# Layer 3's two product groups moved next to each other, in the previous block's second half and behind the second block product of the next scores

## The chip, the cores and the metric

The kernel runs on one core of a Trainium2 chip. The core has TensorE for matmuls (PE; its weight loads are listed apart as PEld), VectorE (DVE), ScalarE (ACT), GpSimd (POOL) and SyncE (SP), which issues most DMA transfers. The engines run side by side, each through its own list of instructions in order, and wait for one another through semaphores. The metric is the device time of the whole kernel in microseconds (us), the median of some runs.

## What is computed

Eight images of 512 channels and 32x32 = 1024 positions go through four layers. In short (B = 8, C = 512, N = 1024):

```python
# layer 0: attention over channels reduced to 64, scaled by the largest singular value
x = Wv @ (h_x @ (f_x^T g_x / sigma)^T) + bv + x
# layer 1: group norm, then attention over 1024 positions with all 512 channels
h = group_norm(x, 32 groups)
q, k, v = wq @ h, wk @ h, wv @ h
x = x + wp @ (softmax(q^T k / sqrt(512)) applied to v)
# layer 2: attention over 1024 positions with 128 channels
t, p, g = split(W_w @ x)
x = batch_norm(Z_w @ (softmax(t^T p / sqrt(128)) applied to g)) + x
# layer 3: product of signs, then batch norm, residual, two slopes
a  = sign(x + rsign_bias)
Wb = sign(W) * mean(|W|, axis=1)
s  = batch_norm(Wb @ a) + x
t  = s - pr_shift
out = where(t > 0, t, pr_slope * t) + pr_bias
```

Layers 0 to 2 are computed in f32; the signs of layer 3 are f16.

## The kernel before

A first phase computes layer 0's small matrices for all images and folds weights together (`wu` from wq and wk, `wo` from wv and wp). Then the function `fast` is called once for each image, in the order 6, 7, 0 to 5 (`order`). One call does, on 128 partitions and in halves of 512 positions (`half(0)`, `half(1)`):

1. `scores1`: layer 1's scores and their exponentials, four rows of blocks
2. `make_v`, `values1`: layer 1's values and the attention's output
3. `project2`, `scores2`, `values2`, `close2`: layer 2. Next to it runs `make_u`, which already computes `ut`, a factor of the next image's scores
4. `leave`: layer 3 and the output, one half at a time

**Products of seven terms.** Large products are done with seven instead of eight block products (`seven`, lines 333 to 375). With the left factor's blocks A and the right factor's blocks B, the terms come in this order, one step of the generator each: A11·B11, S2·T2, S3·T3, S1·T1, A12·B21, S4·B22, A22·T4. The S and T are sums and differences of blocks, made on DVE beforehand (`sums_of`, `differences_of`). Each term is two f32 matmuls of 128x512 (four records in the trace) into a PSUM bank through line 388. A12·B21 adds to the bank of A11·B11, S4·B22 to that of S1·T1, A22·T4 to that of S3·T3, each once the first content has been taken out. The terms of one product make 7 steps. `scores1` has 4 such products, so the steps of its loop in `fast` count k from 0 to 27; `make_u` has 2.

In the trace these terms have the names of their factors. In `scores1`, the left factor `ut` gives `ut` for its own blocks (A11, A12, A22, and S3, which is written over A21) and `us` for S1, S2, S4; the right factor gives `h` for its own blocks and T3, and `hs` for T1, T2, T4. So the first steps of `scores1` read `ut,h` (A11·B11), `us,hs` (S2·T2), `ut,h` (S3·T3), `us,hs` (S1·T1), `ut,h` (A12·B21), then `us,h` (S4·B22) and `ut,hs` (A22·T4). Those of `make_u` read `wu`, `su` in place of `ut`, `us`.

**Where `us` comes from.** The last step of `make_u` calls `done`, which calls `sums_of` on `ut`: S1 (line 314), S2 (line 317), S3 (line 318) and S4 (line 319), four DVE instructions of 128x1024. Their inputs are evicted from PSUM by lines 341 (ACT), 345 and 347 (DVE), with an add on POOL (line 360).

**Layer 3.** `leave` (lines 679 to 752) makes for each half the signs `sg` (four ACT instructions, line 686) and then, for j = 0 and 1, one product group: four f16 matmuls of 128x512 into one bank (line 698). Two output channels are packed in each sum; ACT and DVE take them apart (line 709 on ACT, 710 and 711 on DVE), scale and add the residual (line 719, DVE), apply the two slopes (lines 741 and 742 on ACT, 749 on DVE), and two 256 KB transfers leave through SP. The generator yields once after each j; with `stop=True` it also yields after the signs.

**Where the groups stand.** In `fast`, half 0 goes through a loop with one step of `make_u` after each j (`fill()`), then `close2` of half 1 (line 675 on PE, line 677 on DVE), then half 1's signs:

```python
            for _ in leave(env, xt, dst, [0]):
                fill()
            close2(xt, att, 1)
            rest3.append(leave(env, xt, dst, [1], stop=True))
            next(rest3[0])
```

Half 1's two groups are left for the next image's scores. There, at k = 0, 2 and 4, one step of the waiting generator is taken; the third finds its end, and the next image's load is issued:

```python
            if rest3 and k % 2 == 0:
                if next(rest3[0], "end") == "end":
                    rest3.pop()
```

While `rest3` holds the generator, no step of the other background work (`chore`, layer 0's chains of small products, lines 1029, 1030 and 1061, in the first three images) is taken. The last image (`more` false) does its layer 3 in another way and isn't touched, nor is the first image's `scores1`, where `rest3` is empty. So there are seven changes from one image to the next with two groups of half 0 before them and two groups of half 1 after.

**The order on the engines.** PE's order is roughly the program's. A planner, which knows estimated durations, may move instructions between neighbours on each engine where no dependence forbids it. PSUM has 8 banks, which all these steps share (`bank`).

Of the kernel before, what the change touches and what calls it, by code (L numbers as in the profile page):

```python
# [85 lines left out]
def kernel(  # L86
# [36 lines left out]
    def bank():  # L123
        return psum["bank"].tile([P, HF], F32, tag="bank", name="bank")
# [9 lines left out]
    def load_x(b, split=False):  # L134
        t = xpool.tile([P, CC, N], F32, tag="x", name="xt")
        src = x[b].rearrange("(cc p) n -> p cc n", p=P)
        for cc in range(CC):
            for ns in [half(h) for h in range(NH)] if split and not cc else [slice(0, N)]:
                nc.sync.dma_start(out=t[:, cc, ns], in_=src[:, cc, ns])
        return t  # L140
# [164 lines left out]
    def quarters_of(t, rows, cols):  # L305

        return [t[:, rows[k], cols[m]] for m in range(2) for k in range(2)]

    def sums_of(a, more, queued=False):

        a11, a12, a21, a22 = a
        s1, s2, s4 = more
        tt = nc.vector.tensor_tensor
        first = tt(s1, a21, a22, ALU.add)
        if queued:
            tc.keep_in_program_order(first)
        tt(s2, s1, a11, ALU.subtract)  # L317
        tt(a21, a11, a21, ALU.subtract)
        tt(s4, a12, s2, ALU.subtract)
        return {"A11": a11, "A12": a12, "A22": a22, "S1": s1, "S2": s2, "S3": a21, "S4": s4}  # L320
# [147 lines left out]
    def split_h(env, ht):  # L468
        hs = env["big"].tile([P, 3, 2, HF], F32, tag="hs", name="hs")
        b = [ht[:, chunks[k], half(n)] for k in range(2) for n in range(2)]  # L470
        return differences_of(b, [hs[:, i] for i in range(3)])
# [44 lines left out]
    def scores1(env, hb, ua, es):  # L516

        scale = float(C) ** -0.5
        esum = env["small"].tile([P, N], F32, tag="esum", name="esum", bufs=1)
        for i in range(NTH):  # L520
            lo, hi = (env["e"].tile([P, N], F32, tag="e", name="e") for _ in range(2))
            es[i], es[NTH + i] = lo, hi
            term = product_of(
                lambda a, b, q, k: hb[b][:, k, bass.ts(i, P)],
                lambda a, b, q, k: ua[a][:, k, :],
            )

            yield from seven(
                term, lo[:, half(0)], hi[:, half(0)], lo[:, half(1)], hi[:, half(1)], exp=scale
            )  # L530
            nc.scalar.activation(lo[:, half(1)], lo[:, half(1)], AF.Exp, scale=scale)
            nc.scalar.activation(hi, hi, AF.Exp, scale=scale)
            if i == 0:
                nc.vector.tensor_tensor(esum, lo, hi, ALU.add)
            else:
                nc.vector.tensor_tensor(esum, esum, lo, ALU.add)
                nc.vector.tensor_tensor(esum, esum, hi, ALU.add)
        es.append(esum)
# [327 lines left out]
    def entering(n):  # L866

        b = order[n]
        f = load_f(b)

        def steps():
            while b // 2 not in ready:
                next(behind)
            if b % 2 == 0:
                for i in (b, b + 1):
                    pvs[i] = weights0(i)
            yield
            yield from enter(resident[b], f, pvs.pop(b), 2 if n else CC)

        return steps()  # L880

    rest3 = []
    verdict = []

    def fast(env, n, hb, ua):


        b = order[n]
        xt = resident.pop(b)
        more = n + 1 < B  # L890
        ahead = iter(())
        count = [0]

        def chore(every):
            count[0] += 1
            if count[0] % every == 0:
                next(behind, None)

        es = [None] * NT
        for k, _ in enumerate(scores1(env, hb, ua, es)):  # L900
            if rest3 and k % 2 == 0:
                if next(rest3[0], "end") == "end":
                    rest3.pop()
                    if more and order[n + 1] not in resident:
                        resident[order[n + 1]] = load_x(order[n + 1])
            if n == 0 and k == 2:
                weights["o"] = sums_of(quarters_of(wo, chunks, cols2), [so[:, i] for i in range(3)], True)
            if n == 0 and k == 6:
                tp = quarters_of(sbw["tpg"], chunks, [slice(0, P), slice(P, 2 * P)])
                weights["tp"] = sums_of(tp, [sp[:, i] for i in range(3)], True)  # L910
            if k == 8 and more:
                ahead = entering(n + 1)


            if k in (10, 13, 20, 27):
                next(ahead, None)
            if not rest3 and k not in (13, 14, 15, 20, 21, 22):
                chore(2)
        esum = es.pop()
        vt = env["big"].tile([P, NT, C], F32, tag="uv", name="vt")  # L920
        for k, _ in enumerate(make_v(hb, vt)):
            if k == 3:
                r = inverse_sums(env, esum, n)
            if k == 5:
                next(ahead, None)
            chore(2)
        for _ in ahead:
            pass
        scratch = env["big"].tile([P, 3, N], F32, tag="us", name="scratch")
        got = []  # L930
        steps = iter(())
        for k, _ in enumerate(values1(env, xt, vt, es, r, scratch)):
            chore(2)
            if k == 5 and more:
                nxt = resident[order[n + 1]]
                hb = split_h(env, normal(env, nxt))
        signs = None
        if more:
            steps = make_u(env, hb, got)
        else:  # L940
            signs = unpacked(env)

        def fill(k=1):
            for _ in range(k):
                next(steps, None)

        made = []
        for k, _ in enumerate(project2(env, xt, made)):
            fill(k > 5)
        tt, pt, gt = made  # L950
        es, esum = scores2(env, pt, tt, lambda t: fill(t % 2))
        banks, r = [None, None], None

        def values2(h, ts):
            if banks[h] is None:
                banks[h] = bank()
            for t in ts:
                mm(  # L958
                    out=banks[h],
                    lhsT=gt[:, t, :],  # L960
                    rhs=es[t][:, half(h)],
                    start=t == 0,
                    stop=t == NT - 1,
                )
            if t == NT - 1:
                att = env["small"].tile([P, HF], F32, tag="half_b", name="att")
                nc.vector.tensor_tensor(att, banks[h], r[:, h, :], ALU.mult)
                return att

        dst = channels(out[b])
        fill()
        values2(0, range(0, 2))
        if more:
            r = inverse_sums(env, esum, B + n)
            values2(0, range(2, NTH))
            att = values2(0, range(NTH, NT))
            values2(1, range(0, NTH))
            close2(xt, att, 0)  # L980
            att = values2(1, range(NTH, NT))
            fill()
            for _ in leave(env, xt, dst, [0]):
                fill()
            close2(xt, att, 1)
            rest3.append(leave(env, xt, dst, [1], stop=True))
            next(rest3[0])
            fill(2)
            for _ in steps:
                pass  # L990
        else:


            r = inverse_rows(env, esum, B + n)
            att = values2(0, range(2, NT))
            values2(1, range(0, 2))
            close2(xt, att, 0)
            values2(1, range(2, 6))
            before, after = leave(env, xt, dst, [0], signs), leave(env, xt, dst, [1], signs)
            count = count_bad(env)  # L1000
            next(count)
            next(before)
            next(before)
            att = values2(1, range(6, NT))
            next(before)
            close2(xt, att, 1)
            for _ in before:
                pass
            next(after)
            next(count)  # L1010
            for _ in after:
                pass

        return hb, got[0] if more else None
# [115 lines left out]
    env = {}  # L1130
# [105 lines left out]
    for b in range(B):  # L1236
        xt = load_x(b) if b else first
# [368 lines left out]
    with tc.If(verdict[0] > 0):  # L1606
        with (
# [5 lines left out]
            env = {"big": big, "e": epool, "small": small}  # L1613
# [4 lines left out]
            for b in range(B):  # L1618
                xt = load_x(b)
# [43 lines left out]
```

## Time and profile before

| | |
|---|---|
| time, median of 3 runs | 1902.76 us (1902.47 to 1903.66) |
| the profiled execution's own time | 1903.3 us |
| its span, first to last instruction | 1901.5 us |
| mean granted TensorE clock | 0.998 |
| f16 matmuls of line 698 on `sw` | 112, 28.7 us busy |
| 600.00 to 639.73 us | PE 39.73 busy, DVE 15.83, ACT 13.48 |
| 639.73 to 653.48 us (half 0's groups to the end of `make_u`) | PE 13.75 busy, DVE 12.52, ACT 10.46 |
| 653.48 to 672.00 us (start of the third image's scores) | PE 18.40 busy, DVE 17.68, ACT 10.63 |

All times inside a run are counted from the start of the span. A line of the timeline names start, length, engine, source line, operation, output and inputs, their shapes, how often it comes in a row, and in brackets how long the engine was idle before and for whom it waited. Matmuls overlap: in such a row the end of the last matmul lies behind the start of the next row, so that PE's time is read from start to start. A line of a group has the count, the busy time, the mean length of one in ns, and behind the second bar the idle time before it with what ended it. The chain of waits goes back from the last instruction to whatever released it each time.

### The profile page before, as it was taken

To read this page: it belongs to the slowest core of one execution; us is meant where nothing else is said; L and a number is where in the kernel's file an instruction comes from. 1 tells how busy PE (TensorE), PEld (TensorE's weight loads), DVE (VectorE), ACT (ScalarE), POOL (GpSimd) and SP (SyncE) were. 2 spreads that over 40 slices of the span, in tenths; PEclk is the share of its full clock that TensorE was granted. 3 is DMA by queue.
4 is the path that set the end of the run, shared out by engine and by line. 5 is a ranking of instruction groups with operands and counts; after the bars stand their busy time and mean duration, and the time that the engine had idled before them with its cause. 6 is when DMAs were issued, how large, how long until landed. Compare 5 with 4: busy or idle time off the path is not lost.

```text
span 1901.5 us, 16368 instructions
## 1 busy us (share of the span) xinstructions
PE 1879.4 (99%) x6178; PEld 976.9 (51%) x6178; DVE 1105.4 (58%) x1762; ACT 510.3 (27%) x811; POOL 224.3 (12%) x176
## 2 busy tenths in 40 slices
PE   9999999999999999999999999999999999999997
PEld 4366456544745447444645446544645455544653
DVE  3256576447664677437664675357753775466547
ACT  2142122134212432035202421134202521234013
POOL 0000101201121011200121001200130011101121
PEclk9999999999999999999999999999999999999999
DMA  8420000002000020002000110002000200000001
GB/s 321 159 78 6 0 7 12 1 16 84 17 1 1 34 72 12 1 12 89 17 1 0 45 61 12 1 22 78 12 0 12 89 12 0 1 33 22 12 0 47
DMA packets 25203, 66.52 MB, mean 35 GB/s; under 512 B 3552, under 2 KB 4764, under 8 KB 24476
## 3 DMA queue, kind: packets, MB, share of 16 engines
q1 hardware_dynamic: 24188, 64.96, 9.5%
q8 instruction: 51, 0.84, 0.2%
q10 hardware_dynamic: 864, 0.43, 0.1%
q14 instruction: 36, 0.29, 0.1%
q0 software_dynamic: 64, 0.00, 0.0%
HBM read 46.44 MB, written 18.94 MB: 34 GB/s over the span
## 4 chain that ended last, share of the span: by engine, by line
PE 92%; DVE 6%; issue 1%; ACT 1%; DMA 0%; POOL 0%; ACTq 0%; DVEq 0%
PE bank L388 42%; PE bank L557 20%; PE bank L958 6%; PE bank L806 6%; PE bank L1248 5%; PE bank L658 3%; PE bank L675 2%; PE bank L412 2%; PE wide L1288 1%; DVE both L749 1%; DVE both L719 1%; PE bank L1029 1%; PE wide L1342 1%; PE bank L1030 1%; PE bank L698 1%; DVE xt L677 1%
## 5 line engine op out<-in xcount | busy, mean ns | idle before, releaser
L557 PE MATMUL bank<-e,vt 128*128 128x512 f32 x768 | 334.2, 593 | 0.0
L557 PEld LDWEIGHTS bank<-e,vt 128*128 128x128 f32 x768 | 144.9, 190 | 174.8 <-issue 173.1
L388 PE MATMUL bank<-ut,h 128*128 128x512 f32 x384 | 182.3, 597 | 0.0
L345 DVE TENSOR_TENSOR e<-bank,e 128x512 f32<-128x512 f32 x128 | 87.7, 685 | 81.9 <-PE bank L388 81.7
L388 PE MATMUL bank<-us,hs 128*128 128x512 f32 x256 | 121.5, 597 | 1.3 <-DVE us L317 0.5
L388 PEld LDWEIGHTS bank<-ut,h 128*128 128x128 f32 x384 | 71.4, 190 | 95.6 <-issue 84.0
L958 PE MATMUL bank<-e,tpg 128*128 128x512 f32 x256 | 114.7, 595 | 0.0
L806 PE MATMUL bank<-tpg 128*128 128x512 f32 x256 | 114.6, 592 | 0.0
L813 ACT ACTIVATE e<-bank 128x512 f32<-128x512 f32 x128 | 76.4, 597 | 128.6 <-PE bank L806 128.6
L388 PE MATMUL bank<-wo,h 128*128 128x256 f32 x384 | 91.8, 382 | 0.0
L388 PE MATMUL bank<-h,wu 128*128 128x512 f32 x192 | 90.3, 593 | 0.7 <-ACT ut L350 0.7
L360 POOL TENSOR_TENSOR e<-e 128x512 f32<-128x512 f32 x32 | 43.3, 1354 | 403.9 <-ACT e L339 238.3
L818 DVE TENSOR_TENSOR esum<-esum,e 128x1024 f32<-128x1024 f32 x48 | 58.8, 1225 | 54.9 <-ACT e L813 54.9
L345 DVE TENSOR_TENSOR vt<-bank,vt 128x512 f32<-128x512 f32 x64 | 44.0, 688 | 68.9 <-PE bank L388 68.5
L806 PEld LDWEIGHTS bank<-tpg 128*128 128x128 f32 x256 | 48.6, 190 | 60.7 <-issue 60.5
L958 PEld LDWEIGHTS bank<-e,tpg 128*128 128x128 f32 x256 | 48.1, 190 | 60.4 <-issue 60.3
L360 POOL TENSOR_TENSOR ut<-ut 128x512 f32<-128x512 f32 x16 | 21.8, 1361 | 473.3 <-ACT ut L341 473.3
L388 PEld LDWEIGHTS bank<-wo,h 128*128 128x128 f32 x384 | 71.6, 190 | 11.5 <-issue 2.5
L388 PEld LDWEIGHTS bank<-us,hs 128*128 128x128 f32 x256 | 47.1, 190 | 54.9 <-issue 48.3
L686 ACT ACTIVATE sg<-xt,rb 128x512 f16<-128x512 f32 x64 | 45.0, 718 | 100.6 <-DVE xt L677 97.1
L1248 PE MATMUL bank<-xt,fg 128*64 128x512 f32 x256 | 59.1, 609 | 4.5 <-DMA fg<-in_w_fg 4.5
L658 PEld LDWEIGHTS bank<-tpg,xt 128*128 128x128 f32 x512 | 59.5, 192 | 7.2 <-issue 7.2
(330 smaller groups left out, 2974.0 us busy)
## 6 DMA issues: line engine op xcount, KB each, us to landing
xt<-in_x SPq DMA_DIRECT2D x55, 512.0 KB
out<-both SPq DMA_DIRECT2D x63, 256.0 KB
rfull<-r_dram SPq DMA_DIRECT2D x15, 512.0 KB
f_dram<-f SPq DMA_DIRECT2D x8, 256.0 KB
fb<-f_dram SPq DMA_DIRECT2D x8, 256.0 KB
w<-in_w SPq DMA_DIRECT2D x1, 1024.0 KB
q<-in_w_q SPq DMA_DIRECT2D x1, 1024.0 KB
k<-in_w_k SPq DMA_DIRECT2D x1, 1024.0 KB
```

The costliest lines, as they stand in the source:

```text
L345: nc.vector.tensor_tensor(dst, ps, u, ALU.add)
L360: nc.gpsimd.tensor_tensor(c22, c22, c12, ALU.add)
L388: mm(out=ps[:, q * w : (q + 1) * w], lhsT=lt(ka, kb, q, k), rhs=rhs(ka, kb, q, k), start=first and q == 0 and k == 0, stop=last and k == 1 ...
L412: mm(out=ps, lhsT=pv[side(h), bass.ts(oc, P)], rhs=f[side(h), :], start=True, stop=True,)
L557: mm(out=ps, lhsT=a[:, t, bass.ts(r_, P)], rhs=e[t], start=first and t == 0, stop=last and t == NTH - 1, skip_group_check=True,)
L658: mm(out=ps[:, i, :], lhsT=xt[:, cc, bass.ts(4 * h + i, P)], rhs=sbw["tpg"][:, cc, 2 * P : 3 * P], start=cc == 0, stop=cc == CC - 1,)
L686: nc.scalar.activation(sg[:, cc, :], xt[:, cc, half(h)], AF.Sign, bias=rb3[:, cc : cc + 1])
L806: mm(out=ps, lhsT=pt[:, 0, bass.ts(t, P)], rhs=tt[:, 0, half(h)], start=True, stop=True,)
L813: nc.scalar.activation(e[:, half(h)], ps, AF.Exp, scale=float(P) ** -0.5)
L818: nc.vector.tensor_tensor(esum, esum, e, ALU.add)
L958: mm(out=banks[h], lhsT=gt[:, t, :], rhs=es[t][:, half(h)], start=t == 0, stop=t == NT - 1,)
L1248: mm(out=banks[i][side(h), :], lhsT=w0[i][:, cc, :], rhs=xt[:, cc, half(h)], start=cc == 0, stop=cc == CC - 1,)
```

## The change

Two places in `fast` are changed. In the loop over `scores1`, the two groups of half 1 are both taken at k = 1, that is behind S2·T2 of the first row, instead of one at k = 0 (behind A11·B11) and one at k = 2 (behind S3·T3); at k = 4 the generator ends, as before. In the loop over `leave` of half 0, no step of `make_u` is taken after the first group and two after the second. No instruction is added or removed.

```diff
         for k, _ in enumerate(scores1(env, hb, ua, es)):
-            if rest3 and k % 2 == 0:
-                if next(rest3[0], "end") == "end":
+            if rest3 and k in (1, 4):
+                for _ in range(2):
+                    done = next(rest3[0], "end") == "end"
+                if done:
                     rest3.pop()
                     if more and order[n + 1] not in resident:
                         resident[order[n + 1]] = load_x(order[n + 1])
...
             fill()
-            for _ in leave(env, xt, dst, [0]):
-                fill()
+            for i, _ in enumerate(leave(env, xt, dst, [0])):
+                fill(2 * (i % 2))
             close2(xt, att, 1)
```

## The prediction

> **What bounds the kernel now.** I read the page first, then the chain of waits around one change of image, then the timelines of TensorE (PE) and VectorE (DVE) there, then the same place at the other six changes.
>
> From the page:
>
> ```profile
> PE 1879.4 (99%) x6178; PEld 976.9 (51%) x6178; DVE 1105.4 (58%) x1762; ACT 510.3 (27%) x811; POOL 224.3 (12%) x176
> PE 92%; DVE 6%; issue 1%; ACT 1%; DMA 0%; POOL 0%; ACTq 0%; DVEq 0%
> L388 PE MATMUL bank<-us,hs 128*128 128x512 f32 x256 | 121.5, 597 | 1.3 <-DVE us L317 0.5
> ```
>
> PE is busy for 99% of the span and carries 92% of the chain. There is next to nothing to win by shuffling PE work unless PE stands still somewhere, and the third line names such a place: products that read `us` and wait for the DVE sum of line 317. The chain of waits around the change from the second to the third image (start, length, what):
>
> ```profile
> 641.49 0.02 issue
> 641.52 0.44 DVE both L710
> ...
> 653.26 1.23 DVE us L314
> 654.49 0.06 DVE ut L347
> 654.55 0.52 issue
> 655.07 1.22 DVE us L317
> 656.29 0.04 issue
> 656.34 3.70 PE bank L388 x8
> ```
>
> Here the chain leaves PE for 15 us and runs through DVE without a break, from the first eviction of layer 3 (L710) to the sum S2 (L317); 0.05 us after S2 ends (656.28) PE starts S2·T2. The PE timeline at this place (start, length, then the group):
>
> ```profile
> 653.48 1.88 PE L388 MATMUL bank<-ut,h 128*128 128x512 f32 x4
> 655.19 1.03 PE L698 MATMUL bank<-sg,sw 128*128 128x512 f16 x4
> 656.34 1.98 PE L388 MATMUL bank<-us,hs 128*128 128x512 f32 x4
> 658.16 1.88 PE L388 MATMUL bank<-ut,h 128*128 128x512 f32 x4
> 659.88 1.03 PE L698 MATMUL bank<-sg,sw 128*128 128x512 f16 x4
> ```
>
> The ends in a row overlap the next start, so only starts count. A seven-product term takes 1.72 (653.48 to 655.19). A layer 3 group takes 0.86 undisturbed (a later query row: 659.88 to 660.74), and the terms and groups of the first half (639.73, 640.60, 642.31, 643.18) follow each other with no loss between f32 and f16. So 655.19 plus 0.86 is 656.06, and S2·T2 starts at 656.34: PE loses 0.28. The term itself then takes 1.82 instead of 1.72, another 0.10 for starting from rest. In other words, the layer 3 group covers 0.86 of a wait of 1.15 us for S2. The six other changes show the same: groups at 434.43, 872.24, 1081.37, 1289.25, 1498.39, 1706.27 and S2·T2 1.13 to 1.14 later each time.
>
> **What the Trainium skill says.** "TensorE: Matmul & The Clock Gate", Part 2, step 1, says that only weight loads may be pulled ahead and that matmuls stay in program order. The trace agrees: PE stands still before S2·T2 although S3·T3 and later groups follow it. So a group placed behind S2·T2 can't fill the wait. "SBUF — State Buffer", Who interferes with whom, says that a DVE instruction with two SBUF inputs and a GpSimd instruction that reads SBUF exclude each other, the later one blocking fully. The trace agrees: one L749 took 1.17 us at 648.94, beside the POOL add of 648.08, and its neighbour 0.74. "VectorE: DVE Perf Modes", The DRAIN you can't avoid, says that no instruction starts before the pipe is empty, but that one that isn't held starts earlier. The trace shows the second part, as follows.
>
> ```profile
> 643.18 1.41 DVE L719 SCALAR_TENSOR_TENSOR both<-both,sa,xt 128x512 f32<-128x512 f32 x2
> 644.51 0.42 DVE L710 TENSOR_SCALAR both<-both 128x512 f32<-128x512 f32 x1
> 644.96 0.69 DVE L711 SCALAR_TENSOR_TENSOR both<-both,bank 128x512 f32<-128x512 f32 x1
> 645.68 0.75 DVE L719 SCALAR_TENSOR_TENSOR both<-both,sa,xt 128x512 f32<-128x512 f32 x1
> ```
>
> An independent DVE instruction starts 0.08 before the end of the one ahead (643.18 + 1.41 = 644.59, the next at 644.51); one that reads its result starts 0.03 after (644.51 + 0.42 = 644.93, the next at 644.96). A dependence between neighbours costs 0.12.
>
> **Part 1, the first half (`leave` of half 0).** Before, PE runs group, S3·T3, group, S1·T1; after, group, group, S3·T3, S1·T1. The sum of PE's time is the same, the second group starts 1.72 earlier, S3·T3 0.86 later, and `close2` at 644.89 doesn't move. No instruction is added, the order of SP and POOL is the same, and no DMA changes place. Banks suffice: the eighth allocation back from each of these is evicted before. What changes is DVE's order (from the built program): L710, L711, then the second group's L710, L719 twice, L711, L345, L719, instead of L710, L711, L345, L719 twice, L710, L711, L719. The second L710's input is there in time: its ACT step can start 0.04 after the group's end (640.60 + 1.03 = 641.63), takes 0.69, so 642.36, and DVE comes to it at 642.58. Two of the three tight dependences (L710 to L711, L711 to L719) now have other work between them: 2 x 0.12 = 0.24 us less in a stretch in which DVE is full. The rest of the way to S2 keeps its order, and nothing else on it becomes late: L347 at 652.49 moves to 652.25 and needs a product ended at 651.92; the one at 654.41 needs 653.64. So S2 comes 0.24 earlier, S2·T2 at 656.10. Bounds: 0, if POOL holds L749 to the same time; 0.73, if everything but the products vanishes, since the second L347 can't start before 653.68 and it takes 0.66 + 1.22 + 0.05 to S2·T2 (655.61 at the earliest). I take 0.24, as the POOL add is itself behind an L719 that moves by 0.24.
>
> **Part 2, the scores (groups at steps 1 and 1 instead of 0 and 2).** A11·B11 ends its turn at 655.19 as before. Nothing now stands between it and S2·T2, so PE waits from 655.19 to 656.10, 0.91 instead of 0.28. That is 0.86 of cover gone and 0.24 regained, 0.62 lost. The two groups then run behind S2·T2 at full pace; their inputs `sg` are ready at 653.3. There are seven changes of image: 7 x 0.62 = 4.4 us. Nothing later gives this back, as PE has no wait of this size in the rest of an image. Step 4 ends the generator and starts the next load of x as before, so the added wait holds back only PE itself.
>
> **A second wait.** Late in the first row, S4·B22 accumulates into the bank of S1·T1, which ACT must first copy out (L339). In the images without a chain step in between, the order before is A12·B21, A22·T4, S4·B22:
>
> ```profile
> 1298.22 1.88 PE L388 MATMUL bank<-ut,hs 128*128 128x512 f32 x4
> 1299.94 1.88 PE L388 MATMUL bank<-us,h 128*128 128x512 f32 x4
> ...
> 1298.83 0.56 ACT L339 COPY e<-bank 128x512 f32<-128x512 f32 x1
> ```
>
> The copy ends at 1299.39, 0.55 before its user. After, the built order puts half of A22·T4 (0.86) behind S4·B22 in five of the seven images. Counted from S2·T2's start: two groups and four and a half terms (1.82 + 2 x 0.86 + 3 x 1.72 + 0.86) put S4·B22 at 9.56. L339 stands in ACT's queue behind two L709, L741, L741, two L742, L741; the first group ends at 2.85, L709 takes it to 3.57, DVE's L710, L711, L710, L719 to 5.75, and the first L741 to L339 takes 3.3 as now, so its end is 5.80 + 3.3 + 0.56 = 9.66, seen by PE at 9.72. That is 0.16 late, plus 0.10 for the start from rest: 0.26 x 5 = 1.3 us. Bounds: 0 (if I have a queue 0.2 too late) and 2.5 (0.5 each). In the other two images a chain step of 0.6 stands before and covers it.
>
> **Sum.** 4.4 + 1.3 = 5.7 us. The profiled execution took 1903.3 (its span is 1901.5), so 1909.0; against the median of 1902.76 that is 1908.4. What a measurement can tell from no change is about 0.2%, 3.8 us.
>
> **The rivals.**
> 1. Forecast, both waits: 1908.4. For it: S2 is ready 0.05 before its user at all seven places and PE can't pass it.
> 2. Only the first wait, the copy being in time: + 4.4, 1907.1. For it: 0.16 is a small margin over a dozen steps.
> 3. DVE saves nothing, POOL being what holds L749: 7 x 0.86 + 1.3 = + 7.3, 1910.1. Against: the POOL add starts after ACT's L341, which has the same L719s ahead of it.
> 4. DVE saves much more: the blocked L749 (0.43 long) escapes POOL. At its limit (0.73) the loss is 7 x 0.13 = + 0.9, 1903.7, no change that can be told.
> 5. Not slower, even faster: S2 is ready before A11·B11 ends. Then the present loss of 0.28 + 0.10 goes too: 7 x 0.38 = - 2.7, 1900.1. It decides from S2 ending at 655.14, 1.14 earlier than now; the second L347 forbids that by 0.42 (its end at 655.56 at the earliest) with the order built, so the dependence would have to be other than I read it. A gain over 0.2% would need still more.
>
> That the change doesn't do what it says is ruled out by the built order: eight f16 products in a row at all fourteen places.
>
> **How the numbers follow.** Chances: 0.58 for the first, 0.13 for the second, 0.10 for the third, 0.13 for the fourth (or anything else that ends within 3.8 of before), 0.06 for the fifth and what else could make it faster by over 0.2%. The first three are slower by over 0.2%, 0.81 together; the fourth is the same. The range goes from 1905.6 (a part of case 4, S2 0.45 earlier with no second wait: 7 x 0.41 = 2.9) to 1910.1, case 3.
>
> **What would show it.** Right: S2·T2 starts 0.8 to 1.0 after A11·B11's turn ends, at seven places, waiting for DVE L317, then groups in rows of eight; five waits for ACT L339 before `us,h`; L710 followed directly by another group's L710 on DVE. Wrong: S2 ending more than 0.5 earlier against the layer 3 groups of the first half, or PE losing time elsewhere.

## The result, and the profile after

The changed kernel takes 1908.64 us (median of 9 runs, 1908.23 to 1909.64); the kernel before, run beside it, 1903.54 us (9 runs, 1902.47 to 1904.22). The ratio is 1.0029 with a 95% interval of 1.0021 to 1.0037: slower by 5.1 us, with an interval that lies wholly above 0.2%. The profiled execution took 1908.4 us, its span is 1906.5.

The line of the page (section of the costliest groups) that named the wait, in the changed kernel: the idle time before the products that read `us` has grown from 1.3 to 5.8 us, all of it put down to the sum S2 of line 317.

```profile
L388 PE MATMUL bank<-us,hs 128*128 128x512 f32 x256 | 121.5, 597 | 5.8 <-DVE us L317 5.8
```

The PE timeline of the changed kernel at the change from the second to the third image (start, length, group):

```profile
639.68 1.89 PE L698 MATMUL bank<-sg,sw 128*128 128x512 f16 x8
...
653.42 1.88 PE L388 MATMUL bank<-ut,h 128*128 128x512 f32 x4
656.03 1.98 PE L388 MATMUL bank<-us,hs 128*128 128x512 f32 x4 [0.73 <-DVE us L317]
657.85 1.89 PE L698 MATMUL bank<-sg,sw 128*128 128x512 f16 x8
659.58 1.88 PE L388 MATMUL bank<-ut,h 128*128 128x512 f32 x4
```

The f16 groups now stand in rows of eight, at the same pace (657.85 to 659.58 is 1.73, two groups). A11·B11's turn ends 1.72 after 653.42, at 655.14; S2·T2 starts at 656.03. Read from start to start, PE stands for 0.89 us; the 0.73 in brackets is shorter, since the last matmul's drawn end runs 0.16 into the wait. Before it was 0.28. The VectorE side of the changed kernel, timeline of the first half's evictions and of the sum:

```profile
641.46 0.43 DVE L710 TENSOR_SCALAR both<-both 128x512 f32<-128x512 f32 x1 [0.82 <-ACT both L709]
641.92 0.69 DVE L711 SCALAR_TENSOR_TENSOR both<-both,bank 128x512 f32<-128x512 f32 x1
642.53 0.42 DVE L710 TENSOR_SCALAR both<-both 128x512 f32<-128x512 f32 x1
642.87 1.41 DVE L719 SCALAR_TENSOR_TENSOR both<-both,sa,xt 128x512 f32<-128x512 f32 x2
644.19 0.68 DVE L711 SCALAR_TENSOR_TENSOR both<-both,bank 128x512 f32<-128x512 f32 x1
644.79 0.68 DVE L345 TENSOR_TENSOR ut<-bank,ut 128x512 f32<-128x512 f32 x1
...
654.76 1.21 DVE L317 TENSOR_TENSOR us<-us,ut 128x1024 f32<-128x1024 f32 x1
```

From the first L710 to L317 it is 13.30 us, before 13.55 (641.52 to 655.07): 0.25 less. The whole of it is gained before the first L749 (4.58 us behind the first L710, before 4.83), the stretch in which the order is another one, and it is 0.25 there at all seven changes. Only the first L710 and L711 are still tight; behind the second L711, the next L719 now starts with L345 in between.

The second wait is there too. PE and then ACT in the changed kernel, at the change to the fifth image:

```profile
1090.83 1.88 PE L388 MATMUL bank<-ut,h 128*128 128x512 f32 x4
1092.55 1.02 PE L388 MATMUL bank<-ut,hs 128*128 128x512 f32 x2
1093.56 1.98 PE L388 MATMUL bank<-us,h 128*128 128x512 f32 x4
```

```profile
1092.34 0.70 ACT L741 ACTIVATE up<-both,cb 128x512 f32<-128x512 f32 x1
1092.95 0.56 ACT L339 COPY e<-bank 128x512 f32<-128x512 f32 x1
```

Half of A22·T4 (`ut,hs`) should take 0.86; S4·B22 (`us,h`) starts 1.01 after it, 0.05 after the copy of line 339 ends (1093.51). The trace puts 0.16 on this wait, at five changes, and the term it delays takes 1.98 instead of 1.88 in the drawing, another 0.10.

Where the 5 us went can be summed. From the first group of half 0 (418.97 before, 418.32 after) to the end of the span it is 1482.57 before and 1488.22 after: 5.66 us more. To the start of the last matmul alone it is 5.76; what follows that matmul (11.22 us before, 11.12 after) isn't touched by the change. The start of the program, which the change doesn't touch either, was 0.65 shorter in this execution, so the span shows only 5.0. Start to start, PE's stand before S2·T2 adds to 1.93 over the seven changes before and 6.38 after, 4.45 more; the wait for the copy adds 5 x (0.16 + 0.10) = 1.3. Together 5.75, against 5.76 up to the last matmul. No other wait between these points changed by more than 0.1.

### The profile page after: what moved, and what is told of

Same layout as the page of the kernel before. It is cut to its first block, busy times and chain, and to the rows that moved or that the text cites. A ratio compares the mean times of both kernels' runs of the same rounds, so it can differ in the third digit from the quotient of the medians.

```text
span 1906.5 us, 16382 instructions
## 1 busy us (share of the span) xinstructions
PE 1880.3 (99%) x6178; PEld 975.9 (51%) x6178; DVE 1104.6 (58%) x1762; ACT 513.3 (27%) x811; POOL 224.5 (12%) x176
## 4 chain that ended last, share of the span: by engine, by line
PE 92%; DVE 6%; ACT 1%; issue 1%; DMA 0%; POOL 0%; ACTq 0%; DVEq 0%
PE bank L388 42%; PE bank L557 20%; PE bank L960 6%; PE bank L806 6%; PE bank L1250 5%; PE bank L658 3%; PE bank L675 2%; PE bank L412 2%; PE wide L1290 1%; DVE both L749 1%; PE bank L698 1%; DVE both L719 1%; PE bank L1031 1%; PE wide L1344 1%; PE bank L1032 1%; DVE xt L677 1%
## 5 line engine op out<-in xcount | busy, mean ns | idle before, releaser
L345 DVE TENSOR_TENSOR e<-bank,e 128x512 f32<-128x512 f32 x128 | 87.8, 686 | 84.1 <-PE bank L388 84.0
L345 DVE TENSOR_TENSOR vt<-bank,vt 128x512 f32<-128x512 f32 x64 | 44.1, 689 | 68.8 <-PE bank L388 68.5
```

The costliest lines, as they stand in the source:

```text
L345: nc.vector.tensor_tensor(dst, ps, u, ALU.add)
```

## The experiments

All ratios are to the kernel before, run on the same chip beside them (1903.12 us for the first four runs, 1903.10 for the last two).

**Part 1 alone** (half 0's groups side by side, the scores as before):

```diff
-            if rest3 and k in (1, 4):
-                for _ in range(2):
-                    done = next(rest3[0], "end") == "end"
-                if done:
+            if rest3 and k % 2 == 0:
+                if next(rest3[0], "end") == "end":
```

Expected:

> Part 1 alone: the groups of half 0 back to back, those of half 1 at steps 0 and 2 of the scores as before. My account: S2 ends 0.24 us earlier at each of the seven changes (two tight dependences on VectorE gone), the group behind A11.B11 still covers 0.86, so the 0.28 of waiting before S2.T2 falls to about 0.04: 7 x 0.24 = 1.7 us faster than the kernel before (0.9991), ratio to it between 0.9985 and 0.9995; no wait of S4.B22 for the copy of line 339. Rival (part 1 itself costs, by a bank or by S3.T3 coming 0.86 later): slower than before by 1 us or more. Rival (the add on GpSimd holds the L749 beside it, nothing is saved): the same as before, S2.T2 still 1.14 behind the group.

Measured: 1901.33 us, ratio 0.9991 (0.9983 to 0.9999), 1.8 us faster. PE timeline of this kernel:

```profile
653.41 1.88 PE L388 MATMUL bank<-ut,h 128*128 128x512 f32 x4
655.13 1.03 PE L698 MATMUL bank<-sg,sw 128*128 128x512 f16 x4
656.01 1.98 PE L388 MATMUL bank<-us,hs 128*128 128x512 f32 x4
657.84 1.88 PE L388 MATMUL bank<-ut,h 128*128 128x512 f32 x4
```

S2·T2 starts 0.88 after the group instead of 1.15, and 0.86 of that is the group itself: 0.02 of waiting is left of 0.28. So this part, which the changed kernel contains, is a gain, and the loss sits in the scores. From the first group to the last matmul the profile has 1.52 us less than before: 1.78 less in front of S2·T2 at the seven changes, and 0.28 lost again where one step of a chain (line 1061, at 449.29) comes late.

One thing isn't as I had called it: S2·T2 still takes 1.98 (its second matmul 0.10 late) although PE hardly stood. So the 0.10 isn't for starting from rest. The weight loads (PEld) show where it comes from. Here are the first two loads of S2·T2 in this kernel:

```profile
656.01 0.30 PEld L388 LDWEIGHTS bank<-us,hs 128*128 128x128 f32 x2 [0.35 <-DVE us L317]
```

And here in the kernel with both groups ahead of S2·T2 (its PE timeline is shown further down), where nothing waits:

```profile
1082.95 0.41 PEld L388 LDWEIGHTS bank<-us,hs 128*128 128x128 f32 x2
```

The weight load of the first matmul waits for S2 too. In this kernel it starts together with its matmul (656.01), the second load 0.11 behind it (656.12), and the second matmul 0.43 behind that load (656.55). In the other kernel the first load starts 0.21 ahead of its matmul (1083.16), so the second load starts with that matmul, and the second matmul follows 0.43 later (1083.59). What is late by 0.10 is thus the second load, pushed back by the first. This is read from the traces; no run changed it alone.

**Part 2 alone** (half 0 as before; A12·B21 of the first row pinned on PE, to keep the changed kernel's order):

```diff
-            for i, _ in enumerate(leave(env, xt, dst, [0])):
-                fill(2 * (i % 2))
+            for _ in leave(env, xt, dst, [0]):
+                fill()
...
+                    if pin and ka == "A12" and k == 0:
+                        tc.keep_in_program_order(made)
```

Expected:

> Part 2 alone: half 0 as before, both groups of half 1 at step 1; A12.B21 of the first row is pinned behind S1.T1 on TensorE, so that the order is that of the changed kernel. My account: S2 comes as late as in the kernel before, the whole cover of 0.86 is gone: S2.T2 starts 1.14 to 1.15 after the turn of A11.B11 ends, 7 x 0.86 = 6.0, and with the wait of S4.B22 for the copy (5 x 0.26 = 1.3) 7.3 us slower than the kernel before (1.0038), about 2 us slower than the change. Rival (part 1 saves nothing): the same time as the change, 1.0029.

Measured: 1910.81 us, ratio 1.0040 (1.0026 to 1.0053), 7.7 us slower. PE and VectorE timelines of this kernel:

```profile
654.01 1.88 PE L388 MATMUL bank<-ut,h 128*128 128x512 f32 x4
656.86 1.98 PE L388 MATMUL bank<-us,hs 128*128 128x512 f32 x4 [0.97 <-DVE us L317]
```

```profile
655.59 1.21 DVE L317 TENSOR_TENSOR us<-us,ut 128x1024 f32<-128x1024 f32 x1
```

PE stands from 655.73 to 656.86, 1.13, and starts 0.06 after S2: the whole wait with no cover. Over the seven changes this is 7.97 us, 1.58 more than in the changed kernel, and the wait for the copy is there five times as well. The medians of the two parts add up, -1.8 and +7.7, to 5.9, about what the change does (5.1).

**Both groups ahead of S2·T2** (k = 0 instead of 1):

```diff
-            if rest3 and k in (1, 4):
+            if rest3 and k in (0, 4):
```

Expected:

> As the change, but both groups of half 1 at step 0, ahead of S2.T2. My account: two groups (1.72) cover more than the 0.91 that PE would wait, so no wait for S2 at all and no start from rest: 7 x 0.38 = 2.7 us faster than before by this alone. But in the order built, ACT's copy of line 339 stands behind all eight steps of the two groups; S4.B22 would wait 0.3 to 0.5 for it, up to seven times (2 to 3.5 us). Together between 2.5 us faster and 1 us slower than before (0.9987 to 1.0005), and 4 to 7 us faster than the change. Rival (what costs is that two groups stand in a row, not that they stand behind S2.T2): as slow as the change, 1.0025 or more.

Measured: 1903.83 us, ratio 1.0005 (0.9997 to 1.0013): 4.4 us less than the changed kernel (each against the kernel before that ran beside it), no different from before. That two groups stand in a row costs nothing by itself. PE timeline of this kernel:

```profile
1079.72 1.88 PE L388 MATMUL bank<-ut,h 128*128 128x512 f32 x4
1081.44 1.89 PE L698 MATMUL bank<-sg,sw 128*128 128x512 f16 x8
1083.16 1.88 PE L388 MATMUL bank<-us,hs 128*128 128x512 f32 x4
...
1091.75 1.08 PE L388 MATMUL bank<-ut,hs 128*128 128x512 f32 x2
1093.06 1.98 PE L388 MATMUL bank<-us,h 128*128 128x512 f32 x4 [0.23 <-ACT e L339]
```

No wait before S2·T2 at all, and the term takes 1.88, without the 0.10. But S4·B22 starts 1.31 after half of A22·T4 instead of 0.86. The copy it needs stands in ACT's queue behind all eight steps of layer 3 here; five times 0.39 and 0.10, 0.06 each time on A22·T4, and single waits of 0.4 and 0.2 on A22·T4 at the two changes with chain steps take the gain back.

**Both groups behind the first row** (k = 6; the load of x and the chain steps still from k = 4):

```diff
-            if rest3 and k in (1, 4):
-                for _ in range(2):
-                    done = next(rest3[0], "end") == "end"
-                if done:
-                    rest3.pop()
-                    if more and order[n + 1] not in resident:
-                        resident[order[n + 1]] = load_x(order[n + 1])
+            if rest3 and k == 4 and more and order[n + 1] not in resident:
+                resident[order[n + 1]] = load_x(order[n + 1])
+            if rest3 and k == 6:
+                for _ in range(3):
+                    next(rest3[0], "end")
+                rest3.pop()
...
-            if not rest3 and k not in (13, 14, 15, 20, 21, 22):
+            if (not rest3 or k >= 4) and k not in (13, 14, 15, 20, 21, 22):
```

Expected:

> As the change, but both groups of half 1 behind the first row's last step (step 6), the load of x and the chain steps still from step 4. My account: PE waits for S2 just as in the change (0.9 us from the turn of A11.B11, seven times, 4.4 us over before), but ACT's copy of line 339 isn't behind layer 3's steps any more, so the second wait (1.3 us) is gone: 1.0023 to before, 1.3 us less than the change. Rival (the second wait costs nothing, the 5 us are all from the first): the same as the change within 0.5 us. Rival (the loss comes from layer 3's ACT and VectorE steps crowding the first row): back to the time of before.

Measured: 1909.79 us, ratio 1.0034 (1.0021 to 1.0048). The first wait is as expected (6.37 us over the seven changes), and in the first row the copy is in time. But I missed that the second row comes under the same layer 3 steps: there S4·B22 waits for its copy three times (0.16 and 0.10 each), and at the first change A22·T4 of a row waits 0.77 for an eviction by VectorE. The second wait was moved, not removed, and the 1.3 us less than the change that I expected didn't come (from the first group to the end 1488.41, 0.18 more). What this run does show is that crowding in the first row isn't the loss: with the first row empty of layer 3, the 0.89 before S2·T2 stay.

**The changed kernel with S4·B22 behind the whole of A22·T4**, in the scores' first row of every image:

```diff
+        if swap:
+            term(pd, "A22", "T4", False, True)
+            yield
+            term(pc, "S4", "B22", False, True)
+            plus(vc, b1, c21, c12)
+            plus(vd, b2, c21, c21)
+            yield
+            return
...
+                    if pin and ka == "S4" and k == 0:
+                        tc.keep_in_program_order(made)
```

Expected:

> The change, with the last two terms of the scores' first row in the other order on TensorE (A22.T4 whole, then S4.B22, pinned), in all images. My account of the second wait (S4.B22 comes 0.16 too early for ACT's copy of line 339 because only half of A22.T4 stands between): with the other half there it is 0.86 later, so no PE time before us,h is put down to L339 any more, in any image, and 5 x 0.26 = 1.3 us of the change's 5.1 are gone: 1.0020 to the kernel before, range 1.0014 to 1.0026; the wait for S2 stays at 0.9 seven times. Rival (the second wait is made up for later, or only moves to another place as in the run with the groups behind the first row): the same as the change, 1.0026 to 1.0030.

Measured: 1907.36 us, ratio 1.0023 (1.0015 to 1.0031). PE and ACT timelines of this kernel, at the same place as shown for the changed kernel (the matmuls of line 388 stand in line 396 here):

```profile
1093.00 1.88 PE L396 MATMUL bank<-ut,hs 128*128 128x512 f32 x4
1094.72 1.88 PE L396 MATMUL bank<-us,h 128*128 128x512 f32 x4
```

```profile
1093.40 0.56 ACT L339 COPY e<-bank 128x512 f32<-128x512 f32 x1
```

The copy ends at 1093.96, S4·B22 starts at 1094.72, and nothing waits; the term takes 1.88. No wait for line 339 is left at any change. From the first group to the end it is 1486.59, 1.64 less than in the changed kernel: the 1.3 of the second wait, 0.13 less before S2·T2, and 0.19 behind the last matmul (10.94 us there, 11.12 in the changed kernel), where the swap changes nothing. The medians alone (0.8 us less, each against its own kernel before, with overlapping intervals) wouldn't settle it; the trace does.

**Both: groups ahead of S2·T2 and the swap** (the diff with k = 0 and the diff of the swap together).

Expected:

> Both groups of half 1 at step 0, ahead of S2.T2, half 0 as in the change, and the last two terms of the first row swapped as in the other run. My account: no wait for S2 (2.7 us under before, by place), and the 0.39 + 0.10 that S4.B22 waited for the copy, five times, is gone too, so 0.9986 to the kernel before, 1900.5, at best a little faster than the run with half 0 alone (0.9991). A22.T4 now needs the eviction of S3.T3 by VectorE, which stands behind two L749: up to 0.1 a time. Rival (the total of PE's waits in the first row is set by VectorE's and ACT's work there, and a wait taken away at one place comes back at the next): 1.0000 to 1.0005 as without the swap.

Measured: 1901.86 us, ratio 0.9992 (0.9984 to 1.0001). From the first group to the end it is 1480.66, as long as with part 1 alone (1480.67) and 1.91 less than before; up to the last matmul it is 1.66 less. Neither wait is left; A22·T4's 0.06 for an eviction, five times, and its single waits at the two changes with chain steps (0.4 and 0.2, with up to 0.1 each on the matmul behind) make up what is missing to the 2.7. The rival (what is taken away at one place comes back at the next) holds for a part only. Two versions thus come out below the kernel before, by 1.8 us (part 1 alone) and 1.2 us (this one) in the medians; only part 1 alone has an interval clear of 1, and by little.

## Why the prediction was right

- **The first wait.** Forecast: S2·T2 at 656.10, 0.91 of standing instead of 0.28, 4.4 us in seven changes. Measured 656.03, 0.89, and 4.45 us. The two halves of that term were shown apart: with no saving on VectorE, the wait was 1.13 to 1.15 (part 2 alone); with the saving and the cover, 0.02 (part 1 alone). The 4.45 contains 0.16 of one change that isn't explained (below); without it the term would be 4.29.
- **The saving on VectorE.** Forecast 0.24, from two dependences between neighbours of 0.12 each. Measured 0.25 from L710 to L317, all of it in the reordered stretch; S2·T2 comes 0.26 earlier behind A11·B11 in part 1 alone. The L749 beside POOL still took 1.17 us (648.63), but POOL's add moved along (647.76 after, 648.08 before), so the third rival fell.
- **The second wait.** Forecast 0.16 + 0.10, five times, 1.3 us; the copy's end was set 9.66 after S2·T2's start. Measured 0.16 + 0.10 five times, and 1093.51 less 1083.85 is 9.66. The run with the swap removes it. That the end was hit to 0.01 is in part luck: the prediction itself allowed this term 0 to 2.5 us.
- **The sum.** Forecast 5.7 on the profiled execution. Measured 5.66 between the first group and the end. The medians differ by 5.1, and the interval of their ratio (4.0 to 7.0 us) takes in both. The start of the program is uneven: in the eight profiles the first group comes between 418.3 and 419.5.
- **What I had wrong without harm:** the 0.10 as the price of starting from rest. It is there with a wait of 0.02 as well, and the traces put it on the weight load that waits too. Before S2·T2 it cancels in the difference, and on S4·B22 it has the forecast size; but it is also the main reason why part 1 alone doesn't gain the full 2.7 us.
- **Not explained:** at the change to the fourth image S2·T2 stood 1.05 instead of 0.89, since S2 came 0.16 late: the first L347 on VectorE started 0.07 us behind the end of the instruction ahead of it instead of 0.08 before, and the profile doesn't say for what it waited. It was so in the changed kernel and in the run with the groups behind the first row, and in no other.

## What to carry to other kernels

On an engine that runs in order and is full, work that looks free to move may be the cover of someone else's wait: before moving it, find the wait that it lies in, and subtract only what the move itself makes ready earlier. Leave in front of the waiting instruction at least as much work as the wait is long; and follow the evictions of what is put there on the other engines too, since what they push back in a queue (here one copy on ACT) can hold the full engine again half a dozen terms later. A change of two parts should be run in its two parts: here one gained 1.8 us and the other lost 7.7.

## What the runs showed of the hardware

- f32 and f16 matmuls follow each other on TensorE with no loss: groups of four or eight f16 matmuls take 216 ns each from start to start, in all the orders with f32 terms (429 ns for each record) that these runs have.
- A matmul whose semaphore is set only as PE reaches it, or later, has its successor 0.10 us late, whether it waited 0.02 us (part 1 alone) or 1.1 (part 2 alone): its weight load waits with it and pushes back the next load. In the run with both groups ahead, S2 was ready 0.89 before S2·T2 and nothing is late; the eviction that A22·T4 needs at the change to the fifth image was done 0.17 before, and the successor is 0.06 late.
- On VectorE a neighbour that reads the last result starts 0.03 us after its end, one that waits for nothing 0.08 before the end; putting other work between two such pairs was worth 0.25 us at each of the seven changes.
